# Two of seven softmax-denominator additions and the residual addition moved from VectorE and GpSimd to accumulating DMAs

## The chip, the cores and the metric

The kernel runs on one core of a Trainium2 chip. The metric is the device time of one launch in microseconds. The engines are called by the profile's names: PE (TensorE matrix multiply), DVE (VectorE), ACT (ScalarE), POOL (GpSimd, which also issues DMAs) and SP (which issues most DMAs).

## What is computed

Two graph layers run over x with 16 batches, 1024 nodes and 256 channels, all in float32. Only layer 0 is touched by the change. Cut to what matters, it is:

```
for each batch b:
    c   = mean of x over channels                       # 1024 values
    W   = adj * f(|c_n - c_m|)                          # 1024 x 1024
    q   = relu((x^T W) * para)                          # queries
    k,v = x @ kv_w                                      # keys, values
    for each of 4 heads:
        p   = exp(q k^T * scale)                        # 1024 x 1024
        out = (p v) / (sum of p over the keys)
    x1  = layernorm(x + out)                            # over channels
```

Layer 1 aggregates x1 with a normalised adjacency, runs two linear layers with batch norms, adds x1 and normalises again.

## The kernel before

The scores are computed transposed, with 128 keys on the partitions. A **unit** is one key block m (0 to 7) for two heads and 512 queries: the function `scores` makes `ps` (128x1024, two heads side by side) on PE, ACT takes the exponential into `p` (L1056), and `outputs` multiplies `p` by the values into two PSUM banks `po` on PE (L1072). Eight units, m = 0 to 7, make a **group**. A batch has four groups, called g0 to g3 below: two pairs of heads, and two halves of the queries each.

The softmax denominator is the sum of p over all keys. `outputs` first adds the eight `p` tiles of a group elementwise into `acc` with seven DVE additions: one at m = 1 (L1080) and six at m = 2 to 7 (L1082). `normalise` later sums `acc` over partitions with a matmul by ones (`den`, L1120) and turns the row into columns through DRAM. At the end of a group ACT copies `po[0]` to `oT` (L1089), DVE adds `po[1]` (L1090) and transposes 32x32 blocks (L1101); this is what frees the two `po` banks for the next group, because the pool has only two. `oT` then travels through DRAM, to come back with queries on the partitions (`o`, L1111). `residual` takes the reciprocal on DVE (L1141), multiplies `o` by it on POOL (L1147) and adds the product to x on POOL (L1148). Once all channels of a batch are done, `statistics_x1` runs bn_stats on DVE (L618, L619), POOL makes the inverse deviation (L591, L593, L623, L624), ACT applies it (L628), and POOL issues the DMA that stores x1 (L1169).

The order of the work on PE, ACT, DVE and SP is written by hand, unit pair by unit pair. A **slot** is two units: `scores` of the new pair, then `outputs` of the previous pair, then other work. A batch has 16 slots, u = 0 to 15, and group g begins at slot 4g. The last pair of a group (m = 6, 7) is therefore multiplied in the first slot of the next group. Between the attention slots stands the work for the next batch:

- u = 0: values and keys (L993, L980), the weights W on ACT and DVE (L825, L830, L834), and `den`.
- u = 1: `residual` for the last pair of heads of the batch before. u = 2 and 3: `statistics_x1` for it.
- u = 4: products p1, p2 and p3 of the graph multiplication x^T W (L883), which is done with seven half-size products (Strassen's scheme). p1's bank is copied by ACT (L906) before p2 adds into the same bank. p3 needs the left-hand sums S that DVE forms in `left_first` (L851 to L853). ACT also applies the layer norm (L628).
- u = 5 to 7: right-hand sums on DVE (L869). u = 8: products p6, p7, p5, p4, and `den` for the first pair of heads.
- u = 11: `residual` for the first pair of heads.

POOL's order is not written by hand: the framework places its instructions when the program is built.

The pool `pp` holds four p tiles of 4 KB per partition. The file also holds a `general_path`, which runs only when denominators leave a safe range; here it doesn't run.

Of the kernel before, what the change touches and what calls it, by code (L numbers as in the profile page):

```python
# [10 lines left out]
F32 = mybir.dt.float32  # L11
I32 = mybir.dt.int32
AF = mybir.ActivationFunctionType
ALU = mybir.AluOpType
# [4 lines left out]
P = 128  # L19
HALF = 512  # L20
# [495 lines left out]
def fast_path(  # L516
# [19 lines left out]
    nc = tc.nc  # L536
    B, N, C = x.shape
    H = 4
    D = C // H
    NCH = N // P  # L540
# [5 lines left out]
    const = ctx.enter_context(tc.tile_pool(name="const", bufs=1))  # L546
# [13 lines left out]
    def tile_s(name):  # L560
        return psum["s"].tile([P, N], F32, tag="s", name=name)
# [4 lines left out]
    def tile_o(name):  # L566
        return psum["o"].tile([P, HALF], F32, tag="o", name=name)
# [165 lines left out]
    with (  # L733
        tc.tile_pool(name="l0c", bufs=1) as l0c,
        tc.tile_pool(name="qkv", bufs=2) as qkv,
        tc.tile_pool(name="pp", bufs=4) as pp,
        tc.tile_pool(name="accp", bufs=2) as accp,
        tc.tile_pool(name="rdp", bufs=1) as rdp,
        tc.tile_pool(name="op", bufs=2) as op,
        tc.tile_pool(name="osp", bufs=1) as osp,  # L740
        tc.tile_pool(name="xsp", bufs=1) as xsp,
    ):
# [300 lines left out]
        def scores(i):  # L1043
            b, pr, qh, m = units[i]
            qT, kT = st[b]["qT"], st[b]["kT"]
            ps = tile_s(f"ps_{i}")
            for kh in range(2):
                for hd in range(2):
                    r = slice(hd * D, (hd + 1) * D)
                    ks = slice(m * P + kh * D, m * P + (kh + 1) * D)  # L1050
                    nc.tensor.matmul(  # L1051
                        ps[kh * D : (kh + 1) * D, hd * HALF : (hd + 1) * HALF], kT[r, pr, ks],
                        qT[r, pr, qh * HALF : (qh + 1) * HALF], start=True, stop=True,
                    )
            p = pp.tile([P, N], F32, tag="p", name=f"p_{i}")
            nc.scalar.activation(p, ps, AF.Exp)  # L1056
            A[i] = p

        def outputs(i):
            b, pr, qh, m = units[i]  # L1060
            s, p = st[b], A.pop(i)
            if m == 0:
                G[b, pr, qh] = {
                    "po": [tile_o(f"po_{i}_{kh}") for kh in range(2)],
                    "acc": accp.tile([P, N], F32, tag="acc", name=f"acc_{i}"),
                }
            g = G[b, pr, qh]
            for hd in range(2):
                h = 2 * pr + hd
                for kh in range(2):  # L1070
                    r = slice(kh * D, (kh + 1) * D)
                    nc.tensor.matmul(  # L1072
                        g["po"][kh][hd * D : (hd + 1) * D, :], s["v"][r, m, h * D : (h + 1) * D],
                        p[r, hd * HALF : (hd + 1) * HALF], start=(m == 0), stop=(m == NCH - 1),
                    )
            def sums():
                if m == 0:
                    g["p0"] = p
                elif m == 1:
                    nc.vector.tensor_add(g["acc"], g.pop("p0"), p)  # L1080
                else:
                    nc.vector.tensor_add(g["acc"], g["acc"], p)  # L1082

            if i < len(units) - 1:
                sums()
            if m == NCH - 1:
                k = (b * PAIRS + pr) * 2 + qh
                g["oT"] = op.tile([P, HALF], F32, tag="oT", name=f"oT_{k}")
                nc.scalar.copy(g["oT"], g["po"][0])  # L1089
                nc.vector.tensor_add(g["oT"], g["po"][1], g["oT"])  # L1090
                if (b, pr) != (B - 1, PAIRS - 1):
                    squares(b, pr, qh)
            if i == len(units) - 1:
                for k in (1, 2):
                    scale_adjacency(k)
                sums()

        def squares(b, pr, qh):
            k = (b * PAIRS + pr) * 2 + qh
            oS = osp.tile([P, HALF], F32, tag="oS", name=f"oS_{k}")  # L1100
            nc.vector.transpose(oS, G[b, pr, qh]["oT"])  # L1101
            nc.sync.dma_start(o_d[k].rearrange("q i j d -> (q i) (j d)"), oS)
            rows_of.append((squares_to_rows, (b, pr, qh)))
# [34 lines left out]
        def residual(b, pr, qh):  # L1138
            g, s = G.pop((b, pr, qh)), st[b]
            k = (b * PAIRS + pr) * 2 + qh  # L1140
            nc.vector.reciprocal(r_all[:, k], g["col"])  # L1141
            r = r_all[:, k].unsqueeze(3).to_broadcast([P, 4, 2, D])
            xs = s["x"][:, 4 * qh : 4 * qh + 4, pr * P : (pr + 1) * P]
            if (b, pr) != (B - 1, PAIRS - 1):
                o = g["o"].rearrange("p n q d -> p n (q d)")
                oh = o.rearrange("p n (h d) -> p n h d", d=D)
                nc.gpsimd.tensor_tensor(oh, oh, r, ALU.mult)  # L1147
                nc.gpsimd.tensor_tensor(xs, xs, o, ALU.add)  # L1148
                return
            pt = tile_s(f"poT_{k}")[:, H0]  # L1150
            for j in range(4):
                nc.tensor.transpose(
                    pt[:, j * P : (j + 1) * P], g["oT"][:, j * P : (j + 1) * P], ident
                )
            o = op.tile([P, 4, 2, D], F32, tag="o", name=f"o_{k}")
            nc.vector.tensor_mul(
                o, pt.rearrange("p (n h d) -> p n h d", h=2, d=D), r
            )
            nc.gpsimd.tensor_tensor(xs, xs, o.rearrange("p n h d -> p n (h d)"), ALU.add)
# [20 lines left out]
        wl = {}  # L1180
        dg = const.tile([P, 7, NCH], F32, name="dg")
        rows, diag, colsum, deg, dinv = dg[:, 0], dg[:, 1], dg[:, 2], dg[:, 4], ncol[:, 0, :NCH]
        scr = const.tile([P, P], F32, name="scr")

        def load_weights():
            t = xTp.tile([P, CC, N], F32, tag="xT", name="wl")
# [29 lines left out]
                )  # L1216

        def adjacency_diagonal():
            for n in range(NCH):
                nc.vector.scalar_tensor_tensor(  # L1220
                    scr, adj_s[:, n, n * P : (n + 1) * P], 1.0, ident,
                    op0=ALU.mult, op1=ALU.mult, accum_out=diag[:, n : n + 1],
                )
# [39 lines left out]
        def scale_adjacency(m):  # L1263
            nc.vector.scalar_tensor_tensor(
                aht[m], aht[m], dinv[:, m : m + 1], aht["row"], op0=ALU.mult, op1=ALU.mult
            )
# [43 lines left out]
        with tc.manual_schedule(  # L1310
# [33 lines left out]
            def back(j):  # L1344

                for i in bursts[j]:
                    outputs(i)
                b, pr, qh, m = units[bursts[j][-1]]
                if m == NCH - 1 and qh == 1:
                    sums.append((normalise, (b, pr)))  # L1350
                    for q in range(2):
                        full.append((residual, (b, pr, q)))
                    if pr == PAIRS - 1:
                        for f in (statistics_x1, finish_x1):
                            for ns in (range(NCH // 2), range(NCH // 2, NCH)):
                                late.append((f, (b, ns)))
# [24 lines left out]
            for j in range(len(bursts)):  # L1381
# [37 lines left out]
                elif u == 4:  # L1419
                    p = st[b + 1]["graph"]["p"]  # L1420
# [7 lines left out]
                elif u == 8:  # L1428
                    p = st[b + 1]["graph"]["p"]
                    p[6]()  # L1430
                    run(next_first, 1)
                    run(sums, 1)
                    if b == B - 2:
                        adjacency_diagonal()
                        for n in range(6):
                            adjacency_rows(n)
                    p[7]()
                    p[5]()
                    p[4]()
                elif u < 8:  # L1440
                    st[b + 1]["graph"]["between"](u)
                else:
                    if u == 9 and b + 2 < B:
                        load_squares(b + 2, 0)
                    if u == 11:
                        run(full, 2)
                    if u == 12:
                        run(next_first, 1)
                        if b + 2 < B:
                            load_squares(b + 2, 1)  # L1450
                    if u == 15:
                        run(next_first, 1)
                    run(next_side, 1)
# [556 lines left out]
def kernel(tc: tile.TileContext, *args):  # L2010


    with tc.tile_pool(name="flag", bufs=1, space=DRAM) as flag:
        good_d = flag.tile([1, 1], I32, name="good_d")
        fast_path(tc, *args, good_d)
        good = tc.nc.values_load(good_d[0:1, 0:1], min_val=0, max_val=2 * P)
        with tc.If(good < 2 * P):
            general_path(tc, *args)
# [30 lines left out]
```

## Time and profile before

| | us |
|---|---|
| median of three runs | 2445.71 (2445.69 to 2445.86) |
| the profiled execution, its own time | 2446.41 |
| its span in the profile | 2444.6 |
| PE busy | 2411.5 (99%) |
| DVE busy | 1862.8 (76%) |
| ACT busy | 1238.3 (51%) |
| POOL busy | 475.7 (19%) |
| layer 0's attention, all batches | to about 1592 |
| one batch, from its p1 to the next batch's p1 (660.37 to 757.06) | 96.69 |

The span is what the profiler saw between first and last instruction; the 1.8 us that separate it from the execution's time lie around the program. In the rows of a timeline a number such as "x16" says that so many instructions were merged into the row. A float32 matmul shows as two records, so a unit's four score matmuls are eight records. The ends of PE rows are modelled, so two rows in a row overlap a little: the distance between starts is the true cost.

### The profile page before, as it was taken

How to read it: one execution, taken by the hardware profiler on the slowest of the kernel's cores; microseconds unless marked ns; L12 is line 12 of the kernel's file. 1: busy time of each engine (PE TensorE's matmuls, PEld its weight loads, DVE VectorE, ACT ScalarE, POOL GpSimd, SP SyncE). 2: the span in 40 equal slices, each digit the busy share in tenths (PEclk: the TensorE clock that was granted, in tenths of full speed). 3: DMA queues.
4: the chain of work that ended last, by engine and by line, in shares of the span. 5: the costliest groups of instructions: out<-in, count | busy, mean ns of one | idle time of the engine just before them, and what ended most of it. 6: DMA issues, size and time to landing. Idle time of an engine off the chain costs nothing.

```text
span 2444.6 us, 32834 instructions
## 1 busy us (share of the span) xinstructions
PE 2411.5 (99%) x12422; PEld 1029.6 (42%) x12422; DVE 1862.8 (76%) x2570; ACT 1238.3 (51%) x1545; POOL 475.7 (19%) x486
## 2 busy tenths in 40 slices
PE   9999999999999999999999999999999999999997
PEld 5343443443434434434334343344444444444455
DVE  5688878878888888788788888956566566478978
ACT  7376675765765756657647667421110111045568
POOL 0021122111311211122112112422122122010026
PEclk9999999999999999999999999999999999999999
DMA  5124232332232332322322327221222222165559
GB/s 164 40 42 85 57 49 70 70 53 68 38 83 54 48 84 56 53 70 56 63 62 44 83 49 97 82 103 70 96 92 78 94 86 86 69 241 172 172 210 343
DMA packets 423175, 221.99 MB, mean 91 GB/s; under 512 B 361568, under 2 KB 394848, under 8 KB 414560
## 3 DMA queue, kind: packets, MB, share of 16 engines
q1 hardware_dynamic: 417648, 168.94, 28.4%
q0 software_dynamic: 4832, 50.34, 4.9%
q8 instruction: 99, 1.62, 0.3%
q14 instruction: 68, 0.56, 0.1%
q10 hardware_dynamic: 528, 0.52, 0.1%
HBM read 136.06 MB, written 83.69 MB: 90 GB/s over the span
## 4 chain that ended last, share of the span: by engine, by line
PE 86%; DVE 9%; ACT 3%; DMA 1%; issue 1%; POOL 0%; POOLq 0%; DVEq 0%
PE ps L1051 18%; PE po L1072 18%; PE pgb L883 7%; PE b_agg L1556 4%; PE pga L883 4%; PE c_agg L1556 4%; PE pk L980 4%; PE b_o L1763 3%; PE pv L993 3%; PE a_agg L1556 2%; PE b_h L1588 2%; PE pgd L883 2%; PE pgc L883 2%; PE a_o L1763 2%; PE c_o L1763 2%; PE c_h L1588 2%
## 5 line engine op out<-in xcount | busy, mean ns | idle before, releaser
L1056 ACT ACTIVATE p<-ps 128x1024 f32<-128x1024 f32 x512 | 497.6, 1021 | 183.7 <-PE ps L1051 130.1
L1082 DVE TENSOR_TENSOR acc<-acc,p 128x1024 f32<-128x1024 f32 x384 | 500.1, 1302 | 54.2 <-ACT p L1056 29.3
L1051 PE MATMUL ps<-qT,kT 64*64 64x512 f32 x4096 | 488.1, 592 | 0.3 <-ACT p L1056 0.3
L1072 PE MATMUL po<-p,v 64*64 64x512 f32 x4096 | 485.3, 589 | 0.0
L1147 POOL TENSOR_TENSOR o<-o,r_all 128x512 f32<-128x512 f32 x62 | 94.8, 1538 | 1090.8 <-DVE r_all L1141 1052.5
L1072 PEld LDWEIGHTS po<-p,v 64*64 64x64 f32 x4096 | 158.2, 133 | 281.3 <-issue 274.3
L1051 PEld LDWEIGHTS ps<-qT,kT 64*64 64x64 f32 x4096 | 151.4, 133 | 286.8 <-issue 249.2
L834 DVE SCALAR_TENSOR_TENSOR wg<-wg,adj_s 128x1024 f32<-128x1024 f32 x128 | 149.4, 1217 | 16.5 <-ACT wg L830 16.5
L825 ACT ACTIVATE wg<-crow,ccol 128x1024 f32<-128x1024 f32 x128 | 146.8, 1147 | 0.5 <-DMA crow<-c 0.5
L830 ACT ACTIVATE wg<-wg 128x1024 f32<-128x1024 f32 x128 | 136.0, 1062 | 0.9
L980 PE MATMUL pk<-xT,kvw_s 128*128 128x512 f32 x256 | 121.8, 598 | 3.1 <-ACT drow L1126 3.1
L993 PE MATMUL pv<-kvw_s,xT 128*128 128x256 f32 x512 | 124.0, 385 | 0.0
L993 PEld LDWEIGHTS pv<-kvw_s,xT 128*128 128x128 f32 x512 | 94.9, 190 | 50.0 <-issue 13.4
L893 ACT ACTIVATE qT<-qT 128x512 f32<-128x512 f32 x60 | 37.3, 629 | 149.8 <-DVE qT L896 145.2
L883 PE MATMUL pgb<-wg,S 128*128 128x512 f32 x240 | 111.0, 605 | 0.0
L883 PE MATMUL pga<-wg,x 128*128 128x512 f32 x240 | 109.6, 599 | 0.7 <-ACT qT L906 0.7
L1556 PE MATMUL a_agg<-ahT,x1l 128*128 128x512 f32 x240 | 108.1, 593 | 0.7 <-ACT agg L1298 0.7
L1148 POOL TENSOR_TENSOR x<-x,o 128x512 f32<-128x512 f32 x62 | 107.8, 1748 | 2.3
L1556 PE MATMUL b_agg<-aT,x1S 128*128 128x512 f32 x240 | 107.9, 592 | 0.0
L654 ACT COPY p_agg<-a_agg 128x512 f32<-128x512 f32 x15 | 8.8, 586 | 183.3 <-PE a_agg L1556 183.3
L690 POOL TENSOR_TENSOR x1S<-x1l 128x512 f32<-128x512 f32 x15 | 19.0, 1264 | 352.3 <-PE c_agg L1556 349.0
L1080 DVE TENSOR_TENSOR acc<-p,p 128x1024 f32<-128x1024 f32 x64 | 77.4, 1209 | 7.5 <-ACT p L1056 7.5
(230 smaller groups left out, 3511.8 us busy)
## 6 DMA issues: line engine op xcount, KB each, us to landing
h<-hw POOLq DMA_DIRECT2D x16, 2048.0 KB, 6.7
hl<-h SPq DMA_DIRECT2D x32, 1024.0 KB
x<-x POOLq DMA_DIRECT2D x16, 1024.0 KB, 4.2
x1l<-x SPq DMA_DIRECT2D x16, 1024.0 KB
xf<-x SPq DMA_DIRECT2D x16, 1024.0 KB
o<-oS SPq DMA_DIRECT2D x62, 256.0 KB
o<-o SPq DMA_DIRECT2D x248, 64.0 KB
x<-in_x_dram SPq DMA_DIRECT2D x15, 1024.0 KB
```

The source lines that it names most:

```text
L825: nc.scalar.activation(w, s["crow"], AF.Abs, bias=s["ccol"][:, n : n + 1])
L830: nc.scalar.activation(w, w, AF.Tanh, scale=0.5)
L834: nc.vector.scalar_tensor_tensor(w, w, 1.0, adj_s[:, n, :], op0=ALU.subtract, op1=ALU.mult)
L883: nc.tensor.matmul(ps, left, right, start=(start and i == 0), stop=(i == NCH // 2 - 1), skip_group_check=True,)
L980: nc.tensor.matmul(ps, kvw_s[:, c, kc * P : (kc + 1) * P], s["xT"][:, c, hs], start=(c == 0), stop=(c == CC - 1),)
L993: nc.tensor.matmul(pt[:, j * C : (j + 1) * C], s["xT"][:, c, n * P : (n + 1) * P], kvw_s[:, c, C : 2 * C], start=(c == 0), stop=(c == CC - 1),
L1051: nc.tensor.matmul(ps[kh * D : (kh + 1) * D, hd * HALF : (hd + 1) * HALF], kT[r, pr, ks], qT[r, pr, qh * HALF : (qh + 1) * HALF], start=Tr ...
L1056: nc.scalar.activation(p, ps, AF.Exp)
L1072: nc.tensor.matmul(g["po"][kh][hd * D : (hd + 1) * D, :], s["v"][r, m, h * D : (h + 1) * D], p[r, hd * HALF : (hd + 1) * HALF], start=(m = ...
L1082: nc.vector.tensor_add(g["acc"], g["acc"], p)
L1556: nc.tensor.matmul(ps, left, right, start=(start and i == 0), stop=(i == NCH // 2 - 1), skip_group_check=True,)
L1763: nc.tensor.matmul(ps, left, right, start=(start and i == 0), stop=(i == 1), skip_group_check=True,)
```

## The change

In each group, the tile of m = 2 comes from a pool `ppb` of its own with one buffer, and is called `pb`. The tiles of m = 4 and m = 5 are added into `pb` by two accumulating DMAs issued from POOL (source p, destination pb, both 128x1024 in SBUF). The tiles of m = 1, 3, 6 and 7 are added into `acc` on DVE as before, and a last DVE addition after m = 7 adds `pb` to `acc`. `pp` keeps its four buffers for the other seven tiles.

In `residual`, for all groups but those of the last pair of heads, the multiplication by the reciprocal goes from POOL to DVE, and the addition to x becomes an accumulating DMA issued from POOL (128x4x128, 256 KB).

To make room, `oT` has one buffer instead of two (the very last one borrows a buffer of `o`), and the scratch tile `scr` shares a buffer with `drow`.

```diff
+        tc.tile_pool(name="ppb", bufs=1) as ppb,
...
+        tc.tile_pool(name="otp", bufs=1) as otp,
...
-            p = pp.tile([P, N], F32, tag="p", name=f"p_{i}")
+            pool, tag = (ppb, "pb") if m == 2 else (pp, "p")
+            p = pool.tile([P, N], F32, tag=tag, name=f"p_{i}")
             nc.scalar.activation(p, ps, AF.Exp)
...
                 elif m == 1:
                     nc.vector.tensor_add(g["acc"], g.pop("p0"), p)
+                elif m == 2:
+                    g["pb"] = p
+                elif m in (4, 5):
+                    nc.gpsimd.dma_start(g["pb"], p, accum_op=ALU.add)
                 else:
                     nc.vector.tensor_add(g["acc"], g["acc"], p)
+                if m == NCH - 1:
+                    nc.vector.tensor_add(g["acc"], g["acc"], g.pop("pb"))
...
-                g["oT"] = op.tile([P, HALF], F32, tag="oT", name=f"oT_{k}")
+                very_last = k == 4 * B - 1
+                pool, tag = (op, "o") if very_last else (otp, "oT")
+                g["oT"] = pool.tile([P, HALF], F32, tag=tag, name=f"oT_{k}")
...
-                nc.gpsimd.tensor_tensor(oh, oh, r, ALU.mult)
-                nc.gpsimd.tensor_tensor(xs, xs, o, ALU.add)
+                nc.vector.tensor_tensor(oh, oh, r, ALU.mult)
+                nc.gpsimd.dma_start(xs, o, accum_op=ALU.add)
...
-        scr = const.tile([P, P], F32, name="scr")
...
+            scr = rdp.tile([P, P], F32, tag="drow", name="scr")
```

In the changed program as built, POOL's instructions for one batch (slots u = 1 of one batch to u = 1 of the next) stand in this order; "waits" names the engines or DMAs whose signals the instruction waits for:

```
rs_l  <- mv_l            waits DVE        (L591, statistics of the batch before)
rs_l  <- rs_l ^ -0.5                      (L593)
nm_l  <- mv_l * rs_l                      (L623)
pb(g0) += p4  DMA        waits ACT, PE, DMA
nm_l  <- -nm_l                            (L624)
pb(g0) += p5  DMA        waits ACT, the DMA before
x1 store      DMA        waits ACT
pb(g1) += p4  DMA        waits ACT, PE, DVE, DMA
pb(g1) += p5  DMA        waits ACT, the DMA before
x += o        DMA  (two, u = 11)   waits DVE
pb(g2) += p4  DMA        waits ACT, PE, DMA
pb(g2) += p5  DMA        waits ACT, the DMA before
pb(g3) += p4  DMA        waits ACT, PE, DVE, DMA
pb(g3) += p5  DMA        waits ACT, the DMA before
x += o        DMA  (two, u = 1)    waits DVE
```

On ACT, the exponentials of m = 0 and m = 1 of the next group are written into the buffers that p4 and p5 of this group occupied, and each waits for the DMA that reads that buffer. Line numbers after L1056 move down in the changed file: the pb addition is L1091 there, the p DMAs L1087, the residual's multiplication L1158 and its DMA L1159.

## The prediction

> **What bounds the kernel now.** I read the page's busy shares first, then the costliest groups, then the timeline of one steady batch engine by engine, because the change sits inside a batch that repeats fourteen times.
>
> ```profile
> PE 2411.5 (99%) x12422; PEld 1029.6 (42%) x12422; DVE 1862.8 (76%) x2570; ACT 1238.3 (51%) x1545; POOL 475.7 (19%) x486
> L1082 DVE TENSOR_TENSOR acc<-acc,p 128x1024 f32<-128x1024 f32 x384 | 500.1, 1302 | 54.2 <-ACT p L1056 29.3
> L1147 POOL TENSOR_TENSOR o<-o,r_all 128x512 f32<-128x512 f32 x62 | 94.8, 1538 | 1090.8 <-DVE r_all L1141 1052.5
> L1148 POOL TENSOR_TENSOR x<-x,o 128x512 f32<-128x512 f32 x62 | 107.8, 1748 | 2.3
> h<-hw POOLq DMA_DIRECT2D x16, 2048.0 KB, 6.7
> x<-x POOLq DMA_DIRECT2D x16, 1024.0 KB, 4.2
> ```
>
> PE is the bound. DVE is a second engine with 24% of air, and POOL is mostly idle. The last two rows are the only prices of large POOL-issued DMAs that the page gives.
>
> How much can a freer DVE bring? The PE timeline around slots u = 2 to 5 (start, duration, work):
>
> ```profile
> 755.16 1.90 PE L1072 MATMUL po<-p,v 64*64 64x512 f32 x16
> 756.99 3.70 PE L883 MATMUL pga<-wg,x 128*128 128x512 f32 x8
> 760.53 1.88 PE L980 MATMUL pk<-xT,kvw_s 128*128 128x512 f32 x4
> 762.24 3.60 PE L883 MATMUL pga<-wg,x 128*128 128x512 f32 x8
> 765.68 3.60 PE L883 MATMUL pgd<-wg,S 128*128 128x512 f32 x8
> ```
>
> Starts are 1.72 us apart for a pair of units and 3.43 for a graph product. One batch needs 32 such pairs (55.0), seven products (24.0), eight key and value steps (13.8) and two den (1.7): 94.5 of the period 96.69. So at most **2.2 us a batch**, 15 x 2.2 = 33 us in all, can be won in layer 0, even if DVE cost nothing.
>
> [...] The trace's own line is 1.7 + 2.5 per MB. [...]p4's and p5's additions into one pb run one after the other (the listed order has that wait). [...] No accumulating DMA is in this trace. [...]two additions took 3.78 us at 710.61 with POOL adding beside them, and 2.56 elsewhere.
>
> **The change part by part.** *DVE, removed and added.* Per batch eight additions go (8 x 1.30 = 10.4) and with them about 2 us of blocking by POOL; four multiplications of 128x512 come (4 x 0.69 = 2.8). DVE loses about 10 of its 80 us. PE can use little of it: the waits on PE shown for DVE in a batch are each below 1 us. I take 0.5 us a batch as gain, 8 us in all; bounds 0 and 33.
>
> *POOL's arithmetic* (94.8 + 107.8 us) goes. It was off the path except that statistics wait for it: first bn_stats began at 751.61, after the POOL addition ended at 751.6.
>
> *The accumulating DMA of 512 KB*, called D, from issue to visible. Low: as a copy, 1.7 + 1.25 = 2.95. Middle: data at half rate, 1.7 + 2.5 = 4.2. Other DMAs hold 30% of the engines' time in a batch[...]; I take **D = 4.5**. High: 8, if the adder runs at less than half the rate assumed (2.5 becomes 6.3). The residual's DMA (256 KB in 512-byte pieces) by the same rule: 1.7 + 1.25 = 3.0, high 5.
>
> Each group has two D in series, followed by a DVE addition. Queued behind that addition on DVE are the oT addition (frees po), the block transpose, and whatever comes next; on ACT the exponentials of m = 0 and 1 of the next group wait for the same two DMAs, and behind them stand the copies of oT, p1's bank and kT. So a late second DMA stops DVE and ACT together, and PE next. The 62 residual DMAs lie on POOL's queue ahead of the p DMAs of g2.
>
> *g0.* POOL's in-order queue has the first DMA behind the inverse deviation, which waits for all eight bn_stats:
>
> ```profile
> 749.45 2.13 POOL L1148 TENSOR_TENSOR x<-x,o 128x512 f32<-128x512 f32 x1
> ...
> 752.66 1.27 POOL L1148 TENSOR_TENSOR x<-x,o 128x512 f32<-128x512 f32 x1
> 758.57 1.11 POOL L591 TENSOR_SCALAR rs_l<-mv_l 128x8 f32<-128x8 f32 x1 [4.64 <-DVE mv_l L619]
> 759.77 2.68 POOL L593 TENSOR_TENSOR rs_l<-rs_l,mhalf 128x8 f32<-128x8 f32 x1
> 762.53 0.38 POOL L623 TENSOR_TENSOR nm_l<-mv_l,rs_l 128x8 f32<-128x8 f32 x1
> ```
>
> After the change, in the same frame: multiplications end at 748.0 and 748.8; the residual DMAs land at about 751 and 752; eight bn_stats with aggregates (4 x 0.52 each half) end at 755.2; L591, L593, L623 end at 759.5, and p4's DMA goes at **759.6**, although p4 was ready at 748.7. p5's lands at X = 759.6 + 2D. Then ACT: exponential 1.0, oT copy 0.6, p1 copy 0.6; p2 can start at X + 2.25, p3 one product later at X + 5.7 (DVE's pb addition, oT, transpose and left sums, about 5 us, end before that). p3 stood at 765.68. Stall: 2D - 0.4 = **8.6**, in 14 batches: 120.
>
> *g2.* Slots u = 9 to 12, in the frame where u = 9 starts at 701.53: p4 is ready at 707.5, but two residual DMAs stand ahead, waiting for DVE's multiplications (m = 3's addition ends 706.8, multiplications 708.4) and taking 0.65 each to issue (the x1 store's issue row). So X = 709.7 + 2D; exponential, oT copy and oT addition bring po free at X + 2.4. PE wanted it at 717.03. Stall 2D - 4.9 = **4.1**, in 15 batches: 62.
>
> *g1.* p4 ready and pb read by PE at 775.3: X = 775.3 + 2D; exponential, oT copy, oT addition, transpose and L930 (3.7 us) must end by 787.5, so D up to about 4.1 is free. Stall 2(D - 4.1) = **0.8**, 16 groups: 13. *g3.* X = 721.3 + 2D; then exponential, oT copy, oT addition, transpose and v copy (3.7), for which den waits at 732.8; and ACT, which runs nearly without gaps in u = 0, is late. About 1.5 at D = 4.2, and 2D beyond: **2.1**, 15 groups: 31.
>
> Sum: 120 + 62 + 13 + 31 - 8 = **218 us**. The profiled execution took 2446.4 (span 2444.6 plus 1.8 around it), so 2664; the median of the runs is 0.7 lower. I say 2660. *At nothing:* the single oT buffer (its reader, the DVE transpose, follows it at once), scr's sharing, and POOL's issue time, 190 x 0.65 = 124 us on an idle engine; if that cover goes it is in the queue order above. Layer 1 is untouched.
>
> **The rivals.**
> 1. *Slow adder, D = 8.* Stalls 15.6, 11.1, 7.8, 9 per group kind: 218 + 167 + 125 + 135 - 8 = 637, 3080 us. For: no accumulating DMA was seen[...]
> 2. *Cheap adder, D = 3.* Only g0 (5.6) and g2 (1.1) stall: 78 + 16 - 8 = 86, 2530 us. For: all in SBUF, DMA share only 0.01 between 743 and 753 us.
> 3. *Faster.* The freed DVE pulls the statistics forward, so that both DMAs hide; then PE's gaps close, at best 33 us: 2413. It decides at g0's p3: with a residual DMA that costs nothing, bn_stats end at 754.3 and p4's DMA still goes at 758.6, so 2D would have to be under 1.4. A single 1 MB store took 4.2. The case is nearly excluded, unless POOL's order isn't what it seems.
> 4. *No change:* gain and stall cancel, D near 1; as unlikely.
>
> **How the numbers follow.** D from 3.5 to 5.5 (2565 to 2785) I give 0.60, D below it (rival 2) 0.15, above it (rival 1) 0.20, faster 0.03, same 0.02. The range runs from 2510, just under rival 2, to 2950, D about 7. 0.2% is 5 us, about what a measurement of this kernel can tell from no change. Faster 0.03, same 0.02, slower 0.95.
>
> **What would show it.** Right: L1082's count at 192 instead of 384, and pb's addition in the list with idle time before it put to a DMA; ACT's p waiting for DMA; a PE gap of 6 to 10 us before p2 of each batch but the first, and one of some 4 us at the first po of g3; DVE busy down by about 150 us (128 x 1.30 and some 30 of blocking less, 62 x 0.69 more); p's DMA at 4 to 5 us to landing. Wrong: batches still 96.7 us apart, p's DMA issued before L591, or DVE never waiting for pb.

## The result, and the profile after

The changed kernel takes **2920.07 us**, median of four runs (2914.69 to 2925.24), against 2445.72 for the kernel before on the same chip (2445.69 to 2445.86): a ratio of 1.194 (95% interval 1.192 to 1.196), 474 us slower. The profiled execution took 2921.51, its span is 2919.6. The forecast was 2660, 214 us slower. The direction and the mechanism held. The forecast missed more than half of the loss, though 2920 lies within its range of 2510 to 2950.

The page of the changed kernel, busy shares, costliest groups and DMA issues (in a group: busy time and mean ns of one, then the idle time of its engine just before it and what ended most of it):

```profile
PE 2541.5 (87%) x12422; PEld 1062.6 (36%) x12422; DVE 1727.0 (59%) x2504; ACT 1234.0 (42%) x1545; POOL 453.3 (16%) x552
...
L1059 ACT ACTIVATE p<-ps 128x1024 f32<-128x1024 f32 x512 | 502.9, 1022 | 721.1 <-DMA p<-p 545.2
...
L1091 DVE TENSOR_TENSOR acc<-acc,p 128x1024 f32<-128x1024 f32 x64 | 78.4, 1225 | 480.5 <-DMA p<-p 480.4
L1089 DVE TENSOR_TENSOR acc<-acc,p 128x1024 f32<-128x1024 f32 x192 | 234.2, 1220 | 120.0 <-ACT p L1059 110.6
...
p<-p POOLq DMA_DIRECT2D x128, 512.0 KB, 4.6
```

DVE did lose work (1862.8 to 1727.0), but PE, the bound, no longer runs through: it has 378 us of idle time where it had 33, and it is busy 130 us longer with the same 12422 records. Both parts matter. ACT's exponentials waited 545 us for the DMAs between p tiles, DVE's addition of pb 480 us. PE's mean granted clock fell from 0.997 to 0.930.

PE in one steady batch, from its p1 at 701.90 (timeline: start, duration, work; in brackets idle time and what ended it):

```profile
701.90 3.70 PE L885 MATMUL pga<-wg,x 128*128 128x512 f32 x8
705.43 1.88 PE L982 MATMUL pk<-xT,kvw_s 128*128 128x512 f32 x4
718.28 6.71 PE L885 MATMUL pga<-wg,x 128*128 128x512 f32 x8 [10.97 <-ACT qT L908]
724.83 3.60 PE L885 MATMUL pgd<-wg,S 128*128 128x512 f32 x8
...
748.47 3.70 PE L885 MATMUL pgb<-wg,S 128*128 128x512 f32 x8 [1.28 <-DVE qT L932]
...
776.97 1.98 PE L1053 MATMUL ps<-qT,kT 64*64 64x512 f32 x8 [4.04 <-ACT p L1059]
782.01 1.99 PE L1053 MATMUL ps<-qT,kT 64*64 64x512 f32 x8 [3.05 <-ACT p L1059]
783.77 2.91 PE L1075 MATMUL po<-p,v 64*64 64x512 f32 x16
...
803.29 1.93 PE L1131 MATMUL den<-acc,ones 128*32 128x512 f32 x8 [2.67 <-DVE v L1000]
...
828.41 1.98 PE L885 MATMUL pga<-wg,x 128*128 128x512 f32 x4
```

On ACT, the exponential that waited for g0's second DMA, and behind it the copy that p2 waits for:

```profile
716.24 1.02 ACT L1059 ACTIVATE p<-ps 128x1024 f32<-128x1024 f32 x1 [3.76 <-DMA p<-p]
...
717.62 0.60 ACT L908 COPY qT<-pga 128x512 f32<-128x512 f32 x1
```

The batch takes 126.5 us instead of 96.69, 29.8 more, and nearly all of it can be placed by laying the starts beside those of the kernel before:

| place | forecast stall | measured stall | besides: the same work, run slower |
|---|---|---|---|
| g0: p2 starts 16.4 after p1, not 5.3 | 8.6 | 11.1 | p2 takes 6.55 to p3, not 3.43: 3.1 |
| g1: den to the next product 2.6, not 1.0 | 0.8 | 1.6 | |
| g2: first po at p1 + 81.9, not + 72.6 (earlier delays included) | 4.1 | 9.3 | next slot 2.7, not 1.7: 1.0 |
| g3: den 4.5 after pk, not 1.8 | 2.1 | 2.7 | den and the next product: 1.0 |
| gain from a freer DVE | -0.5 | 0 | |
| sum | 15.1 | 24.7 | 5.1 |

The second wait in g2 ends at 782.01; the scores after it take 1.8 us and not the 0.9 of full speed, so some 0.9 of the 9.3 is slow work too.

Over the program, the 14 periods from the first p1 to the last grew by 408.9 us. Before the first it is 1.4. From the last p1 to layer 1's first aggregation it is 59.1 (186.8 against 127.7), of which some 27 belong to g0, g1 and g2 as in any batch, and some 32 to what follows them, the den of g3 and the last batch. The remaining 5.6 us of the span lie after that, in layer 1, and were not followed.

### The profile page after: what moved, and what is told of

It is laid out like the page before. It is cut to its first block, busy times and chain, and to the rows that moved or that the text cites. A ratio compares the mean times of both kernels' runs of the same rounds, so it can differ in the third digit from the quotient of the medians.

```text
span 2919.6 us, 32855 instructions
## 1 busy us (share of the span) xinstructions
PE 2541.5 (87%) x12422; PEld 1062.6 (36%) x12422; DVE 1727.0 (59%) x2504; ACT 1234.0 (42%) x1545; POOL 453.3 (16%) x552
## 2 busy tenths in 40 slices
DMA packets 474343, 305.36 MB, mean 105 GB/s; under 512 B 364608, under 2 KB 429632, under 8 KB 465728
## 5 line engine op out<-in xcount | busy, mean ns | idle before, releaser
L1053 PE MATMUL ps<-qT,kT 64*64 64x512 f32 x4096 | 517.2, 619 | 110.3 <-ACT p L1059 110.3
L1075 PE MATMUL po<-p,v 64*64 64x512 f32 x4096 | 507.3, 613 | 0.0
L1091 DVE TENSOR_TENSOR acc<-acc,p 128x1024 f32<-128x1024 f32 x64 | 78.4, 1225 | 480.5 <-DMA p<-p 480.4
L1089 DVE TENSOR_TENSOR acc<-acc,p 128x1024 f32<-128x1024 f32 x192 | 234.2, 1220 | 120.0 <-ACT p L1059 110.6
L885 PE MATMUL pga<-wg,x 128*128 128x512 f32 x240 | 143.5, 753 | 158.9 <-ACT qT L908 158.9
L1087 POOL DMA_DIRECT2D p<-p x128 | 128.0, 1000 | 765.0 <-ACT p L1059 437.9
L1159 POOL DMA_DIRECT2D x<-o x62 | 81.3, 1539 | 714.2 <-DVE r_all L1152 689.8
L885 PEld LDWEIGHTS pga<-wg,x 128*128 128x128 f32 x240 | 55.5, 243 | 246.1 <-ACT qT L908 171.4
L995 PE MATMUL pv<-kvw_s,xT 128*128 128x256 f32 x512 | 142.6, 428 | 0.0
L995 PEld LDWEIGHTS pv<-kvw_s,xT 128*128 128x128 f32 x512 | 107.4, 215 | 62.6 <-issue 28.1
L1131 PE MATMUL den<-acc,ones 128*32 128x512 f32 x248 | 54.8, 765 | 55.6 <-DVE v L1000 40.5
```

The lines of the kernel that those rows point to most:

```text
L885: nc.tensor.matmul(ps, left, right, start=(start and i == 0), stop=(i == NCH // 2 - 1), skip_group_check=True,)
L995: nc.tensor.matmul(pt[:, j * C : (j + 1) * C], s["xT"][:, c, n * P : (n + 1) * P], kvw_s[:, c, C : 2 * C], start=(c == 0), stop=(c == CC - 1),
L1053: nc.tensor.matmul(ps[kh * D : (kh + 1) * D, hd * HALF : (hd + 1) * HALF], kT[r, pr, ks], qT[r, pr, qh * HALF : (qh + 1) * HALF], start=Tr ...
L1075: nc.tensor.matmul(g["po"][kh][hd * D : (hd + 1) * D, :], s["v"][r, m, h * D : (h + 1) * D], p[r, hd * HALF : (hd + 1) * HALF], start=(m = ...
L1087: nc.gpsimd.dma_start(g["pb"], p, accum_op=ALU.add)
```

## The experiments

Those without a range were run once. The kernel before took 2446.4 to 2447.7 beside them (medians). Where an expectation says rings, it means the 16 DMA engines of the page.

**The sums alone** (the residual on POOL's arithmetic, as before):

```diff
-                nc.vector.tensor_tensor(oh, oh, r, ALU.mult)
-                nc.gpsimd.dma_start(xs, o, accum_op=ALU.add)
+                nc.gpsimd.tensor_tensor(oh, oh, r, ALU.mult)
+                nc.gpsimd.tensor_tensor(xs, xs, o, ALU.add)
```

> Only the sums by DMA; the residual's multiplication and addition stay on POOL as before the change. Theory (the p DMAs, two in series behind POOL's in-order queue, stall DVE and ACT): POOL's arithmetic stands in the same queue and takes longer (6.5 us at u = 11 against about 3 of DMA issue), so g2's pair starts some 7 us later and g0's some 2 us later than in the changed kernel; about 39 us a batch over before instead of 30, so 3000 to 3080 us. Rival (the residual's accumulating DMA, which lands after 5.4 us, is what costs): 2450 to 2600 us.

Measured 2880.26, batches 122 to 126 but for the first. The theory's size missed (it expected more than after); its rival, that the residual's DMAs are the cause alone, fell. p2 starts 15.0 after p1, so the wait of g0 is there without any residual DMA. In g2, however, the first DMA now takes 5.8 us until the second is issued, where the changed kernel needs 9.4. So the residual's DMA is part of the loss: without it the kernel is 40 us faster.

**The residual alone** (all seven sums on DVE):

```diff
-                elif m == 2:
-                    g["pb"] = p
-                elif m in (4, 5):
-                    nc.gpsimd.dma_start(g["pb"], p, accum_op=ALU.add)
                 else:
                     nc.vector.tensor_add(g["acc"], g["acc"], p)
-                if m == NCH - 1:
-                    nc.vector.tensor_add(g["acc"], g["acc"], g.pop("pb"))
```

> Only the residual part: multiplication on DVE, addition by accumulating DMA; all seven sums on DVE as before. Theory (p DMAs cost): bn_stats begin some 2 us later than before, which DVE's slack before p3 nearly holds; within 20 us of before, 2440 to 2465 us. Rival (the residual's DMA is what costs): most of the loss stays, 2700 us or more.

Measured 2455.4 (2454.5 to 2456.93), ratio 1.0034 (1.0021 to 1.0046), as expected. Most steady batches are 96.7 as before, but three in a row (from p1 at 757.66 to 1051.28) take 97.7 to 98.0: p3 starts 4.3 to 4.7 after p2, not 3.43, because DVE finishes its left-hand sums later. By itself this half costs 8 us, some 3.5 of it in these three batches and some 3.5 after the last p1. The single oT buffer is in this kernel too; together with the 96.7 us of the other batches this bears out that it costs nothing. These two kernels also price the DMAs' time on the 16 DMA engines. POOL's queue of the kernel before, of the sums alone and of the residual alone, from the three pages (packets, MB, share of the 16 engines' span):

```profile
q0 software_dynamic: 4832, 50.34, 4.9%
```
```profile
q0 software_dynamic: 23264, 117.46, 16.5%
```
```profile
q0 software_dynamic: 37568, 66.60, 10.8%
```

Share times span, less that of before, over the number of DMAs: (0.165 x 2878.5 - 0.049 x 2444.6) / 128 = **2.77 us** of all 16 engines for a 512 KB addition, and (0.108 x 2453.8 - 119.8) / 62 = **2.34 us** for a residual addition of half the bytes, in 512-byte pieces.

**Half a clock after a wait.** Twelve matmuls with zero weights behind p1 keep PE busy through g0's wait; they add zeros to p1's bank.

```diff
...
                 product(1, pg["a"], True)
+                for _ in range(12):
+                    nc.tensor.matmul(pg["a"][:32], zw, lo(0, H0), start=False, stop=True, ...)
```

> The changed kernel with twelve matmuls of zero weights (added zeros, 10.3 us) behind p1 in each batch, so that PE works on through the wait before p2. Theory (after an idle stretch PE's granted clock is 0.50 for some 6 us, so each stall costs more than its length): p2 takes 3.4 instead of 6.6 us and the batch 3 us less, about 2875 us, although PE does more. Rival (p2 is slow because DVE, ACT and DMAs work beside it): p2 stays at 6.6 and the time at 2915 to 2930 us or above.

Before it, the changed kernel's windows around p2's start and after (start:end, length, busy time of PE, PEld, DVE, ACT and POOL, granted clock, DMA share, GB/s):

```profile
718.00:719.00 1.00, 0.72 (x1) 0.50 (x2) 0.97 (x2) 1.00 (x3) 0.00 (x0) 0.50 0.00 0
...
723.00:724.00 1.00, 1.00 (x2) 0.39 (x2) 0.64 (x2) 0.00 (x0) 0.50 (x1) 0.50 0.52 80
724.00:725.00 1.00, 1.00 (x3) 0.36 (x2) 0.00 (x0) 0.00 (x0) 0.00 (x0) 0.81 1.01 320
```

The clock stands at 0.50 from PE's restart to 724, then rises. The timeline of PE in the padded kernel:

```profile
705.65 10.49 PE L911 MATMUL pga<-wg,zw 128*32 128x512 f32 x24
...
718.53 3.70 PE L887 MATMUL pga<-wg,x 128*128 128x512 f32 x8 [0.47 <-ACT qT L914]
```

p2 starts where it did (16.5 after p1) but takes 3.70 instead of 6.71. The other engines have the same work beside it, so the slow p2 is the restart's clock. The time, 2900.08, fell by 20 and not by the 45 expected: the theory was right on p2 and wrong on the sum. The starts of the two kernels show why. The changed kernel's p2 is not always as slow as in the batch above: from p2 to p3 it took 5.2 to 6.6 us in the fourteen batches that wait, on average 2.4 over the 3.43 of before, not 3.1. With the padding it is 3.54 in every batch, which saves 31 us over the 14 periods. But in the first batch p2 had hardly waited (4.9 us after p1), and there the twelve matmuls themselves put it at 14.8, 10 us later. 31 less 10 is the 21 by which the 14 periods shortened.

**g0's sums on DVE**, the other groups' by DMA:

```diff
...
-                elif m in (4, 5):
+                elif m in (4, 5) and (pr, qh) != (0, 0):
...
```

The same condition stands at the pb tile of m = 2, and the last addition is made only where a group has a pb.

> The changed kernel, but g0's seven sums all on DVE; g1, g2 and g3 keep the two DMAs. Theory (g0 costs 11.1 us of wait and 3.1 us of half clock per batch): 14 x 14 us less, 2700 to 2750 us. Rival (DVE and ACT meet the next late pair instead and the loss moves): above 2850 us.

Measured 2739.14, as expected: p2 starts 5.3 after p1 again, batches take 113 to 119. So g0's pair is worth 181 us. g2 still pays its wait (in the batch from 772.28 its first po starts at p1 + 69.8, the po before it at p1 + 56.5; undisturbed, they are 3.4 apart).

**Longer rows for SP's loads.** Are the 128-byte pieces of xS what holds up g2's first DMA?

```diff
-            src = x[b].rearrange("(j k) (c q i) -> c q k j i", k=SQ, q=NQ, i=SQ)
+            src = x[b].rearrange("(c q k j) i -> c q k (j i)", c=CC, q=NQ, k=SQ)
...
```

> The changed kernel, but the two loads per batch of x in 32x32 squares (128-byte pieces, 512 KB each) are plain loads of the same size with 4 KB rows; the keys and values are then made from reordered x. Theory (g2's pair of DMAs takes 13.9 us instead of 9.7 because it shares the rings with 128-byte pieces): the first of the pair lands after about 5 to 6 us instead of 9, about 4 us less in each of 14 batches, 2850 to 2880 us. Rival (the pair is long because [...]1.9 us of issue): no change, 2910 to 2930 us.

A miss: 2912.96. In the page, packets under 512 B fall from 364608 to 241728, but g2's first DMA keeps its length. POOL in that kernel:

```profile
763.42 1.93 POOL L1088 DMA_DIRECT2D p<-p  x1
772.78 0.86 POOL L1088 DMA_DIRECT2D p<-p  x1 [7.43 <-DMA p<-p]
```

Still 9.4 us. SP's short rows are not the cause.

**The residual wholly on DVE**, so that no residual DMA stands in the DMA engines' queue; POOL's order is left to the framework:

```diff
                 nc.vector.tensor_tensor(oh, oh, r, ALU.mult)
-                nc.gpsimd.dma_start(xs, o, accum_op=ALU.add)
+                nc.vector.tensor_tensor(xs, xs, o, ALU.add)
```

> The changed kernel with the residual's multiplication and addition both on DVE: no residual DMA, and POOL as built has g0's first DMA ahead of L591, its second behind L624. Theory (g2's first DMA takes 9.4 us in the changed kernel because two residual DMAs of 2.3 us each on all rings are ahead of it): g2's first DMA takes 4.6 to 5.8 us and starts when p4 and pb are free; g0's second one is still late by some 4 us; 2690 to 2770 us. Rival (g2's first DMA is long for another reason): it stays at 8 us or more, and 2850 us or more.

Measured 2761.4, as expected, 159 us less. POOL's queue at g2, first in the changed kernel, then in this one:

```profile
765.37 2.62 POOL L1159 DMA_DIRECT2D x<-o  x2 [24.29 <-DVE r_all L1152]
766.97 1.93 POOL L1087 DMA_DIRECT2D p<-p  x1
776.34 0.86 POOL L1087 DMA_DIRECT2D p<-p  x1 [7.44 <-DMA p<-p]
```
```profile
711.23 0.87 POOL L1087 DMA_DIRECT2D p<-p  x1 [24.69 <-PE po L1075]
716.27 0.87 POOL L1087 DMA_DIRECT2D p<-p  x1 [4.17 <-DMA p<-p]
```

9.4 us between the two issues with two residual DMAs ahead, 5.0 without. 4.6 for a pair's own DMA and 2 x 2.34 for the two in front is 9.3: the p DMA was issued in time and stood behind them in the DMA engines. The trace's DMA packets show this directly: here the p DMA's first packet starts 4.0 us after the issue, as the last 512-byte packets of the residual end; elsewhere it is 1.4 (median). The sum fits better than its parts, though. The two in front had a start of 1.6 us, so they explain only 2.6 us of the delay; the other 1.8 are the p DMA's own packets, which took 4.5 us instead of 2.8, and why was not followed.

The 159 us are not the residual DMAs' alone. In this kernel the framework has g0's first addition ahead of L591, where the changed kernel has it behind L623, so the order differs too (p2 starts 10.3 after p1, not 16.4).

**POOL in the order as written.** POOL joins the engines whose order is the program's. Then g0's pair stands ahead of the inverse deviation, and g2's ahead of the residual DMAs.

```diff
-                mybir.EngineType.SP,
+                mybir.EngineType.SP, mybir.EngineType.Pool,
```

> The changed kernel, with POOL's instructions kept in the order in which the code writes them: g0's pair stands ahead of L591 and g2's ahead of the residual's DMAs. Nothing else differs. Theory (the queue order makes the pairs late): g0 loses some 12 us of its 14 and g2 some 6 of its 10, 2640 to 2720 us. Rival (two DMAs in series are late in any order): 2850 us or more.

Measured 2714.94, as expected, 205 us less with the same instructions on every engine. p2 starts 7.4 to 9.2 after p1, batches take 109 to 115 us. The timeline of POOL, first at g0, then at g2:

```profile
626.96 2.63 POOL L1159 DMA_DIRECT2D x<-o  x2 [24.02 <-DVE r_all L1152]
628.61 1.89 POOL L1087 DMA_DIRECT2D p<-p  x1
636.43 0.86 POOL L1087 DMA_DIRECT2D p<-p  x1 [5.93 <-DMA p<-p]
```
```profile
687.52 0.86 POOL L1087 DMA_DIRECT2D p<-p  x1 [24.69 <-PE po L1075]
692.62 0.84 POOL L1087 DMA_DIRECT2D p<-p  x1 [4.24 <-DMA p<-p]
693.24 2.83 POOL L1159 DMA_DIRECT2D x<-o  x2
```

g2's pair now stands ahead of the residual DMAs, 5.1 us between its issues. g0's does not: the residual DMAs of u = 1 are still in front of it, and there it is 7.8.

**Both**, the written order and the residual on DVE, so that a pair has nothing in front of it anywhere:

> POOL in the order as written (the pair of g0 ahead of the inverse deviation) and the residual wholly on VectorE, so that nothing stands in front of a pair's DMAs on POOL or in the rings: the two sums in series are all that is left of the change. Theory (of the 269 us that remained with the written order, the residual DMAs, then behind the pairs, are worth little; the series of two DMAs is worth nearly all): 2670 to 2720, batches 107 to 110. Rival (the residual DMAs still take a large part, by sharing the rings): under 2600.

Measured 2651.29 (2644.75 to 2651.6), ratio 1.083 (1.081 to 1.085), 20 under the expected range: the residual's DMAs were worth 64 us, more than "little" and far from the rival's 115 or more. The expectation had them behind the pairs; ahead of g0's pair they were not. p2 starts 5.3 after p1 in nearly every batch here and takes 3.43, and these two terms make 44 of the 64. The four kernels make a table:

| | residual by DMA | residual on DVE |
|---|---|---|
| POOL's order as the framework has it (not the same in the two) | 2920.07 (the change) | 2761.4 |
| POOL's order as written | 2714.94 | 2651.29 |

In a batch of the last kernel that took 108.4, 11.7 more than before (they take 105.3 to 110.3), g0 is at its old place, g1 loses 1.6, g2 3.8, den of g3 3.1, and the rest, about 3, is den and the slots after a wait running slowly. These are the price of two DMAs in series: the second is issued only when the first has landed (the waits of some 4.2 us for "DMA p<-p" above). No run added the two tiles into two buffers.

**One DMA a group instead of two** (m = 5 back on DVE; POOL's order as the framework has it):

```diff
-                elif m in (4, 5):
+                elif m == 4:
```

> The changed kernel with m = 4 alone added by DMA; m = 5 goes to DVE. Built so, POOL has g0's DMA ahead of L591. Theory (two DMAs in series are what is late): g0, g1 and g3 no longer stall, g2 still waits for its DMA behind the residual's, some 5 us a batch; 2480 to 2560 us. Rival (the first DMA is already late): above 2700 us.

Measured 2462.91, better than expected. The steady batches are 96.7 to 97.9. The expectation had g2's DMA behind the residual's; the framework, with one DMA a group less, placed it ahead:

```profile
613.43 0.85 POOL L1087 DMA_DIRECT2D p<-p  x1 [28.13 <-DMA xS<-in_x_dram]
615.90 2.60 POOL L1159 DMA_DIRECT2D x<-o  x2 [1.61 <-DVE r_all L1152]
```

So this kernel has not the changed kernel's order but, in the steady batches, that of "POOL in the order as written", without the second additions. The fair comparison is with the 2714.94 there, and the 474 us come apart like this: 205 go with the order, 252 more with the second DMA, and 17 are left.

**The pair earlier in the group** (pb = the tile of m = 0, DMAs for m = 1 and 2, pb added after m = 5):

```diff
-            pool, tag = (ppb, "pb") if m == 2 else (pp, "p")
+            pool, tag = (ppb, "pb") if m == 0 else (pp, "p")
...
-                elif m in (4, 5):
+                elif m in (1, 2):
                     nc.gpsimd.dma_start(g["pb"], p, accum_op=ALU.add)
...
```

> The changed kernel with the same number of DMAs, on other tiles: m = 0 is pb, m = 1 and 2 are added by DMA, and pb goes into acc on DVE after m = 5. The pair then has the long stretches in u = 0, 4 and 8 and some 7 us more before anyone waits. Theory (each DMA is cheap where nobody waits for it; only their place costs): within 30 us of before, 2440 to 2480 us. Rival (the DMAs' traffic[...] slows the engines wherever it stands): 2700 us or more.

A miss of some 450 us: 2929.85 (2926.66 to 2937.95), ratio 1.197 (1.195 to 1.199). It lies in the rival's range, but not for the rival's reason. p2 is at 5.3 again, but the waits of that kernel (engine and line, waited for: us, times, longest) say:

```profile
ACT p L1059 <- DMA p<-p: 550.6, 127, 8.4
```

The expectation had looked at the reader of pb alone. The first DMA writes pb, which PE reads for po one slot after it is made (POOL's issue waits for po). And the exponentials of m = 5 and 6 reuse the buffers that the two DMAs read, so all 64 groups pay in the middle, where before only the ends did.

**Is there a gain at all?** One DMA a group, and the residual on POOL as before:

> m = 4 alone added by DMA, and the residual on POOL as before the change: each group has six DVE additions instead of seven and one DMA. Theory (a single DMA is hidden, and e2 and e8 lost their few us to the residual's DMA in the last batch): 2438 to 2450 us, a gain only as far as PE's 2.2 us a batch depend on DVE. Rival (the DMA's place costs even alone, since POOL's arithmetic stands ahead of it in g2): 2460 us or more.

Measured 2450.94 (2448.61 to 2462.36), ratio 1.0019 (1.0010 to 1.0028). From the third on the steady batches are 96.69, exactly as before, with DVE at 1785.1 us of work instead of 1862.8: the freed time bought nothing. Here, too, g2's DMA stands ahead of the residual's work on POOL. The profiled execution is not a typical one: it took 2462.36, one of two of the twelve near 2462, while the others took 2448.6 to 2452.0. In it 13 of the 16 us over before lie between the last p1 and layer 1's first aggregation. The last batch has no products between its slots, and DMAs for layer 1 run beside it: in the kernel before, the DMA share there is 0.47 (1434 to 1500 us) and 0.42 (1500 to 1592), against 0.30 in a steady batch. Where the other ten executions lose their 2 to 5 us is not shown. **The same with the last batch's sums on DVE:**

```diff
...
-                elif m == 4:
+                elif m == 4 and b < B - 1:
...
```

> One accumulating DMA per group (m = 4 only), the residual on POOL as before, and in the last batch all sums on VectorE as before. Theory (a single DMA is fully hidden in the steady batches and the freed VectorE time buys nothing; the 4 us that the one-DMA kernel lost fell in the last batch, where the rings are busy with loads for layer 1): 2445 to 2448, equal to the kernel before. Rival (the loss is spread over the batches, or a freer VectorE is worth something after all): 2450 or more, or under 2443.

Measured 2452.18 (2451.02 to 2453.48), ratio 1.0021 (1.0012 to 1.0030): a miss, since nothing came back. The profiled execution (2451.95) is 5.5 us longer in its span than before. 1.1 of it is there before the first scores (the products at 22.72 us start at 23.78), where the change does nothing yet, and 0.3 in the first batches. 1.9 come in the last batch: ACT waits 2.20 us at 1502 for the DMA of the group before, the last one left, and PE 1.81 us at 1523. The other 2.3 lie in layer 1 and were not settled. No version tried beats the kernel before.

## Why the prediction was right in direction and short in size

- **The mechanism held.** PE waits before p2 for ACT's copy, which stands behind exponentials that wait for the pair's second DMA; the written order took 205 us off, leaving out the second DMA 252 more. Most forecast marks were met: 192 additions at L1089, pb's addition put to a DMA, DVE down by 136 us (150 forecast). What the prediction calls blocking by POOL shows in the mean of DVE's addition acc<-acc,p: 1302 ns before and 1298 with the sums alone, both with POOL's arithmetic in the kernel, 1220 in the changed kernel and 1221 with the residual alone. By what mechanism was not shown. The PE gap before p2 was 10.97, just over the 6 to 10 forecast, and the first po of g3, forecast some 4 us late, came 9.3 late, with PE waiting at the scores ahead of it.
- **D held.** 4.5 forecast, 4.6 median from issue to landing. The half rate in it was the author's assumption, as no DMA of the kernel before adds. Measured, the adding DMA takes 2.77 us of the engines, where the kernel before gives 1.25 for a copy of that size (119.8 us for the 50.34 MB of POOL's queue): 2.2 times as much. The allowance for the other DMAs, from 4.2 to 4.5, was an estimate too: in the batch above the packets of the pairs of g1 and g3 took 2.8 us, like g0's. So rival 1, the slow adder of D = 8, was not the case, though its 3080 came nearer than the forecast. With nothing ahead of a pair, g2's stall is 3.8 where the forecast had 4.1.
- **The step that failed first: the residual's DMA "by the same rule", 3.0.** Of the two that stand together, the first lands after 4.4 and the second, behind it, after 5.5 (5.4 is the median of all), and each takes 2.34 us of the engines, nearly as much as twice the bytes in long rows. In g0, bn_stats waited for the first and p4's DMA went at p1 + 4.6, not + 2.6: most of the 2.5 us between 8.6 and 11.1. DVE and POOL there:

```profile
697.49 0.43 DVE L618 BATCH_NORM_STATS2 st_l<-x 128x6 f32<-128x256 f32 x1 [2.64 <-DMA x<-o]
```
```profile
705.95 0.20 POOL L623 TENSOR_TENSOR nm_l<-mv_l,rs_l 128x8 f32<-128x8 f32 x1
706.53 0.93 POOL L1087 DMA_DIRECT2D p<-p  x1 [0.37 <-issue]
```

- **The same step in g2.** The prediction counted the residual DMAs ahead of g2's pair by their issue on POOL (2 x 0.65) and not by their transfer. X = 709.7 + 2D should have been D + (D + 2 x 2.34): 4.7 us more, where the issues above differ by 4.3, against the 5.2 us by which 4.1 fell short of 9.3. The 9.4 and 5.0 us and the packets above show it: the p DMA's first packet came 4.0 us after its issue, as the residual's last ones ended.
- **A term was missing: the restart.** The sum took PE at full speed after each wait. In the batch above the granted clock was 0.50 after the gap of 10.97 us at p2, which cost 3.1 us there and 2.0 elsewhere in the batch, and at p2 alone 32 us over the 14 periods. How long it lasts varies: in the batch above to 724, some 6 us of work; p2 to p3 took 1.8 to 3.1 us longer in the fourteen batches, which at a clock of 0.50 is 3.6 to 6.2 us of slow work. At den (803 to 806) the clock was 0.50 after a gap of 2.67 us. The kernel before has it in one place, in layer 1: PE waits 2.98 us until 2355.14, and from 2357 to 2359 its clock is 0.50. The prediction's own gaps, 8.6 and 4.1, are longer than that one.
- **The last batch.** From the last p1 on, the prediction's stalls come to 8.6 + 0.8 + 4.1 + 2.1 + 0.8 = 16.4; 59.1 was measured. Where it had 2.9 for g3 and the last batch, these lost some 32: the last batch's slots follow one another without products, and PE waits 5.25 us at den, 4.76 at the scores, 8.83 at den and 3.96 at the scores (1946, 1968, 1994 and 2018 us).
- **g3** measured 2.7 for 2.1, g1 1.6 for 0.8 (the prediction's own figures give g1 (787.5 - 775.3 - 3.7) / 2 = 4.25 us for a D, so 0.5 and not 0.8). The gain of 0.5 a batch was zero: in the kernel with one DMA a group and the residual on POOL the period doesn't move, so the 2.2 us of PE time that the prediction left open are not DVE's.
- **POOL's arithmetic** of the residual left the path for a DMA of worse latency (an addition on POOL took 1.75 us, the DMA with the residual alone 5.1 from issue to landing); alone, that cost 8 us, and was hidden in all but three steady batches.

By size, from the starts in the traces: the span grew by 475 us where the sum had 218. Of the 257 between them, 206 lie in the 14 periods (g0's wait 37, p2's restart 32, g1 17, g2 and g3 with the slow work after them 113, the gain that did not come 7), 43 after the last p1, 1.4 before the first and 5.6 in layer 1.

The terms are not additive: the order is worth 205 us with the residual DMAs and 110 without, and the residual DMAs 159 and 64, part of it because the framework's order is not the same in the two kernels. Two DMAs in series, with nothing ahead of them and the residual on DVE, cost 205.

## What to carry to other kernels

Before you hand an addition to a DMA, follow its result to the next reader and count everything that is ahead of it, on the issuing engine's queue and in the DMA engines, each DMA ahead by its transfer and not by its issue (2.34 us and not 0.65 for each residual DMA here). Two accumulations into one buffer ran one after the other here, some 5 us from issue to issue with nothing ahead of them: one hid nearly completely, two could not. Where a framework places the instructions of the issuing engine, read the order as built anew for every version: it differed between kernels here that differ in one line. And when a bound PE gets a wait of a few microseconds, add the slow restart, 2 to 3 us after an 11 us gap here, to the wait itself.

## What was not expected of the hardware

- The granted clock stood at 0.50 for about 6 us after an 11 us gap in the batch shown (in others p2's delay speaks for 4 us), and at 0.50 for about 3 us after a gap of 2.67 us at den. With twelve matmuls that filled the first gap, p2 took 3.70 us instead of 6.71.
- An adding DMA of 256 KB in 512-byte pieces cost 2.34 us of the 16 DMA engines, one of 512 KB in 4 KB rows 2.77; from issue to landing 4.4 for the first of two short-piece DMAs, 5.5 for the second, and 4.6 for the long rows (medians). On POOL the issue took 1.00 us on average for the long rows (L1087, 128.0 us for 128) and 1.31 for the short pieces (L1159, 81.3 us for 62), where the forecast had 0.65 for both; POOL, 16% busy, had the air for it.
